# A sum built by its own DMA instead of copied, GpSimd's DMA order fixed, and one transfer for a row of reciprocals, in a two-layer non-local attention kernel

## Chip, cores, metric

The kernel runs on one core of a Trainium2 chip. The metric is the device time of one launch in microseconds, as the median of several runs. Tensor data are float32 throughout.

## What is computed

Two non-local (self-attention) blocks follow each other on `x` of shape 4 x 128 x 96 x 96 (batch, channels, height, width). One block, cut to its core:

```python
# x: (b, 128, 96, 96); CI = 64
g_x     = maxpool2(conv1x1(x, g_w, g_b)).reshape(b, CI, -1).transpose(0, 2, 1)
theta_x = conv1x1(x, theta_w, theta_b).reshape(b, CI, -1).transpose(0, 2, 1)
phi_x   = maxpool2(conv1x1(x, phi_w, phi_b)).reshape(b, CI, -1)
f = einsum('bqc,bck->bqk', theta_x, phi_x)       # 9216 queries x 2304 keys
y = einsum('bqk,bkc->bqc', softmax(f), g_x)
W_y = conv1x1(y, W_w, W_b)                       # then a batch norm with fixed statistics
return W_y * inv + (bn_beta - bn_mean * inv) + x
```

## The kernel before, in words

There are eight blocks (four images x two layers, in `ORDER`). A block's queries are cut into nine pairs of 1024, its keys into 18 tiles of 128. The main loop (L910) runs over 648 steps; one step is two key tiles of one pair, so nine steps make a pair and 18 steps, two pairs, make a cycle. In a step TensorE computes the scores of two key tiles (L592), ScalarE their exponentials with a fixed shift (L597), VectorE adds the exponentials up (L606, for the softmax's denominators), and TensorE multiplies the exponentials of the step before by the values (L614). There are six exponential buffers (`EXPS`).

Into these steps the kernel weaves two other works.

*The keys and values of the next block.* `g` and `phi` need a 1x1 convolution of x and a 2x2 max-pool. They are made in six units of 16 rows per block (class `Unit`, L400), by a scheme that saves multiplications: weights are combined once (`mixed`), and sums of x over halves of the channels and neighbouring rows are built by DMA. Two tiles hold sums, `sums[0]` (called `one`) and `sums[1]` (`two`); "low" and "high" are the partitions 0 to 63 and 64 to 127. `Unit.build` (L413) returns the steps:

- `load`: SP copies x into all of `one` and into `two[high]` (L422, L423);
- `add_one`: GpSimd issues two accumulating DMAs, x into both halves of `one` (L419);
- `load_rest`: SP copies x into `two[low]` (L426);
- an add of `one[high]` into `two[high]` (GpSimd, L419): the third sum;
- `copy_half` (L432): SP copies the second half of `two[high]`'s columns to `self.half`, 64 low partitions in a free part of the tile `stage` (L433), because TensorE shall read one half of the columns from the high and the other from the low partitions at the same time;
- an add of `two[high]` into `two[low]` (GpSimd, L419): the last sum.

TensorE uses these sums in four stages of a unit: `first` (x itself), `second` (L467, reads `two[high]`, first half of the columns) with `second_rest` (L470, reads `self.half`), `third` (reads `one`), `fourth` (reads `two[low]` and x). `second_rest` is emitted in the same step as `second`, after that step's scores and before the values (L946). The multiplications of `second` and `second_rest` both stand on L449, the others on L443.

The steps at which these pieces stand are written by hand. `UNITS` (L44) has the steps of the four stages and `BUILDS` (L45) those of `build`, for even and odd units, counted from the cycle of the unit's pair of units. An even unit builds at 10 to 15 and computes at 15, 16, 18 and 20; an odd one builds at 18 to 23 and computes at 25, 26, 28 and 30.

*The end of a pair.* When all keys of a pair are done, VectorE transposes and reduces the sum of exponentials (`turn`, L655), and `invert` (L670) makes the reciprocals. These are on 32 partitions and have to be spread along rows and over 64 partitions: four DMAs write them as rows into `stage` (L688, 1 KB each), four more broadcast each row over 64 partitions (L693, 64 KB each), all on SP. `normalise` (L703) multiplies by them, `multiply` (L705) projects, and `add` (L714) lets ScalarE add a shift and GpSimd add the result to x by an accumulating DMA (L724). In a cycle of 18 steps `invert` stands at step 13 for the even and at step 6 for the odd pair (`INVERT`), `normalise` at 1 and 10 (`NORM`), and the projection at 3 and 13 (`PROJECT`).

What sets the order: `tc.manual_schedule(engines=...)` (L99 to L101) keeps the program's order for TensorE, VectorE, ScalarE and SP. GpSimd is not in the set, and a scheduler places its instructions. Each engine takes its queue in order, and an instruction that waits holds all behind it. Semaphores carry the waits between engines and for landed DMAs.

```python
def second_rest(self):
    self.part(self.blk.w.mixed[:CI, 2, :], self.half, 1)
...
for i, step in zip(BUILDS[u % 2], unit.build()):
    later(cycle + u // 2 * CYCLE + i, step)
```

Of the kernel before, what the change touches and what calls it, by code (L numbers as in the profile page):

```python
# [17 lines left out]
B, C, CI, H, W = 4, 128, 64, 96, 96  # L18
HW = H * W
NK = (H // 2) * (W // 2)  # L20
QT = 512
# [18 lines left out]
UN = 4 * W  # L40
# [1 line left out]
UB = 2 * UK // 32  # L42
TB = NKT // 2
UNITS = ((15, 16, 18, 20), (25, 26, 28, 30))  # L44
BUILDS = ((10, 11, 12, 13, 14, 15), (18, 19, 20, 21, 23, 23))  # L45
STORE = 3
AFTER = ((1, 1, 2, 4, 5), (1, 2, 2, 3, 4))
THETAS = (6, 5)
# [4 lines left out]
SQ = 32  # L53
# [9 lines left out]
def shifted_blocks(ctx: ExitStack, tc: tile.TileContext, x: bass.AP, layers, out: bass.AP, flag):  # L63
# [24 lines left out]
    nc = tc.nc  # L88
# [8 lines left out]
    ps_misc = ctx.enter_context(tc.tile_pool(name="ps_misc", bufs=2, space=PSUM))  # L97

    engines = {mybir.EngineType.PE, mybir.EngineType.DVE, mybir.EngineType.Activation,  # L99
               mybir.EngineType.SP}  # L100
    ctx.enter_context(tc.manual_schedule(engines=engines))  # L101

    ident = const.tile([P, P], F32, name="ident")
# [10 lines left out]
    stage = const.tile([P, NK], F32, name="stage")  # L114
# [285 lines left out]
    class Unit:  # L400
# [12 lines left out]
        def build(self):  # L413

            low, high = slice(0, CI), slice(CI, P)
            one, two = sums

            def add(dst, src):
                nc.gpsimd.dma_start(out=dst, in_=src, accum_op=ALU.add)  # L419

            def load():
                nc.sync.dma_start(out=one, in_=self.pixels(0, slice(0, P)))  # L422
                nc.sync.dma_start(out=two[high], in_=self.pixels(1, low))  # L423

            def load_rest():
                nc.sync.dma_start(out=two[low], in_=self.pixels(1, high))  # L426

            def add_one():
                add(one[high], self.pixels(0, low))
                add(one[low], self.pixels(1, low))  # L430

            def copy_half():  # L432
                nc.sync.dma_start(out=self.half, in_=two[high, :, UN // 2 :])  # L433

            return (
                load, add_one, load_rest, lambda: add(two[high], one[high]), copy_half,
                lambda: add(two[low], two[high]),
            )

        def both(self, *some):  # L440
            for c in range(2):
# [107 lines left out]
    class Pair:  # L549
# [120 lines left out]
        def invert(self):  # L670

            four = work.tile(
                [SQ, P // SQ, SQ], F32, tag="four", name=f"four_{self.name}", bufs=1
            )
            both = work.tile([SQ, 2, SQ], F32, tag="both", name=f"both_{self.name}", bufs=1)
            for k in range(P // SQ):
                nc.vector.transpose(four[:, k, :], self.parts[ts(k, SQ), :])
            nc.vector.tensor_reduce(
                both[:, 0, :], four.rearrange("p k q -> p q k"), AX.X, ALU.add
            )  # L680
            nc.vector.reciprocal(both[:, 1, :], both[:, 0, :])
            nc.vector.tensor_reduce(notes[:SQ, self.number, :], both, AX.X, ALU.add)
            self.rc = self.halves[:, QT:]
            n = QT // SQ // 2
            first = CI + self.number % 2 * SQ
            for i in range(4):
                row = stage[first + i : first + i + 1, NK - UN :][:, : QT // 2]
                nc.sync.dma_start(  # L688
                    out=row.rearrange("o (b k) -> o b k", k=SQ), in_=both[ts(i, n), 1, :]
                )  # L690
            for i in range(4):
                row = stage[first + i : first + i + 1, NK - UN :][:, : QT // 2]
                nc.sync.dma_start(  # L693
                    out=self.rc[ts(i // 2, CI), ts(i % 2, QT // 2)],
                    in_=row.unsqueeze(1).to_broadcast([1, CI, QT // 2]),
                )

        def add_halves(self):
# [15 lines left out]
        def add(self):  # L714

            cols = ts(self.p, PT)
            here = self.blk.xt[:, cols]
            if self.number < late:
                for h in range(2):
                    nc.scalar.activation(  # L720
                        self.halves[:, ts(h, QT)], self.pss[h], AF.Identity,
                        bias=self.blk.w.shift,
                    )
                nc.gpsimd.dma_start(out=here, in_=self.halves, accum_op=ALU.add)  # L724
            else:
                for h in range(2):
                    dst = here[:, ts(h, QT)]
                    nc.vector.scalar_tensor_tensor(
                        dst, self.pss[h], self.blk.w.shift, dst, op0=ALU.add, op1=ALU.add
                    )  # L730
                self.put()
# [77 lines left out]
    def begin(n):  # L809

        blocks[n].xt = xs[ORDER[n][0]]
        blocks[n].begin_keys()
# [66 lines left out]
    def later(t, step):  # L879
        tails.setdefault(t, []).append(step)  # L880

    for n in range(1, len(blocks)):
        cycle = (n - 1) * NP * NB // CYCLE * CYCLE
        for u in range(NU):
# [5 lines left out]
            if u == 0:  # L890
                later(cycle + BUILDS[0][0], lambda n=n: begin(n))
            for i, step in zip(BUILDS[u % 2], unit.build()):
                later(cycle + u // 2 * CYCLE + i, step)
# [16 lines left out]
    for t in range(total + 1):  # L910
        q, s = 2 * (t // CYCLE), t % CYCLE
        even, odd = pairs[q : q + 2] if t < total else (None, None)
        first, second, take = None, *pending
# [3 lines left out]
        if t in keys:  # L917
            n, i = keys[t]
            first, *pending = blocks[n].chunks(i)
        elif unit:  # L920
            first = (unit.first, unit.second, unit.third, unit.fourth)[stage_of]
            second = unit.second_rest if stage_of == 1 else None
            take = (unit.first_sum, unit.second_sum, unit.third_sum, unit.fourth_sum)[stage_of]
        elif t < total and s == THETAS[q > 0]:
            if q < late:
                first, *pending = thetas(pairs[q + 1 : q + 3])
            else:
                first, take = odd.theta_alone()
# [342 lines left out]
def nonlocal_blocks(tc: tile.TileContext, x: bass.AP, layers, out: bass.AP):  # L1271
    with tc.tile_pool(name="flag", bufs=1) as pool:
        flag = pool.tile([1, 1], I32, name="flag")
        shifted_blocks(tc, x, layers, out, flag)
        bad = tc.nc.values_load(flag[0:1, 0:1])
        with tc.If(bad > 0):
            general_blocks(tc, x, layers, out)
# [30 lines left out]
```

## Time and profile before

| | us |
|---|---|
| median of three runs | 2748.55 (2744.99 to 2748.56) |
| the profiled execution, whole | 2745.14 |
| its span, first to last instruction | 2743.2 |
| TensorE busy | 2527.4 (92%) |
| VectorE busy | 2195.4 (80%) |
| ScalarE busy | 1667.2 (61%) |
| GpSimd busy | 213.5 (8%) |
| mean granted TensorE clock | 0.960 |

The profile is one execution, recorded by the hardware. PE is TensorE, DVE VectorE, ACT ScalarE, POOL GpSimd, SP the engine whose queue issues most DMAs; "PEld" is the loading of weights, which runs beside multiplications, and "SPq" or "POOLq" an engine's queue when it only issues. A tile is named without its number: `stage<-sums` is a transfer from a sums tile into `stage`. The releaser of a wait is inferred from semaphore events, so a wait on several things carries the name of the last. The issue of a DMA and its landing are two events: the row of an SP issue is the time in which SP issues, and the data arrive later. The granted clock is recorded in stretches at 1.00 or 0.50, which carry no reason.

### The profile page before, as it was taken

To read this page: it belongs to the slowest core of one execution; us is meant where nothing else is said; L and a number is where in the kernel's file an instruction comes from. 1 tells how busy PE (TensorE), PEld (TensorE's weight loads), DVE (VectorE), ACT (ScalarE), POOL (GpSimd) and SP (SyncE) were. 2 spreads that over 40 slices of the span, in tenths; PEclk is the share of its full clock that TensorE was granted. 3 is DMA by queue.
4 is the path that set the end of the run, shared out by engine and by line. 5 is a ranking of instruction groups with operands and counts; after the bars stand their busy time and mean duration, and the time that the engine had idled before them with its cause. 6 is when DMAs were issued, how large, how long until landed. Compare 5 with 4: busy or idle time off the path is not lost.

```text
span 2743.2 us, 56475 instructions
## 1 busy us (share of the span) xinstructions
PE 2527.4 (92%) x23391; PEld 1568.1 (57%) x23391; DVE 2195.4 (80%) x2947; ACT 1667.2 (61%) x1836; POOL 213.5 (8%) x244
## 2 busy tenths in 40 slices
PE   9888989889988898988998889898899888999998
PEld 4445544557744565455774456545566545666665
DVE  7777979778777796977876779787788677978877
ACT  5555656556655565755665556565566555666664
POOL 0010001100011000110001100010100110000000
PEclk9999999999999999999999999999999999999999
DMA  5355445443346444546334554444433455433333
GB/s 166 40 73 118 41 49 69 58 55 25 32 63 88 67 54 64 77 58 124 25 31 64 81 70 58 64 74 53 61 25 26 70 79 68 61 41 40 40 41 55
DMA packets 96980, 167.61 MB, mean 61 GB/s; under 512 B 17346, under 2 KB 74060, under 8 KB 96716
## 3 DMA queue, kind: packets, MB, share of 16 engines
q1 hardware_dynamic: 67652, 94.12, 27.9%
q0 software_dynamic: 28896, 69.75, 16.8%
q8 instruction: 185, 3.03, 0.4%
q14 instruction: 79, 0.65, 0.1%
q10 hardware_dynamic: 168, 0.07, 0.0%
HBM read 19.21 MB, written 18.87 MB: 14 GB/s over the span
## 4 chain that ended last, share of the span: by engine, by line
PE 68%; DVE 8%; DMA 7%; SPq 4%; issue 2%; ACT 2%; DVEq 0%; ACTq 0%
PE av L614 32%; PE sc L592 30%; DMA stage<-sums 5%; DVE sum L606 4%; SPq L693 4%; PE unit_ps L443 2%; PE theta_ps L269 2%; PE W_ps L709 2%; ACT exp L597 1%; DMA stage<-both 1%; DMA halves<-stage 1%; PE unit_ps L449 1%; DVE parts L665 1%; SPq L688 1%; DVE turned L664 1%
## 5 line engine op out<-in xcount | busy, mean ns | idle before, releaser
L597 ACT ACTIVATE exp<-sc,nshift 128x1024 f32<-128x1024 f32 x1296 | 1392.0, 1112 | 968.1 <-PE sc L592 929.4
L606 DVE TENSOR_TENSOR sum<-sum,exp 128x1024 f32<-128x1024 f32 x1151 | 1407.7, 1223 | 296.8 <-ACT exp L597 239.1
L592 PE MATMUL sc<-theta,phi 64*64 64x512 f32 x10368 | 1468.8, 593 | 3.0 <-ACT exp L597 2.9
L614 PE MATMUL av<-exp,gT 64*64 64x512 f32 x10368 | 1427.8, 604 | 0.0
L614 PEld LDWEIGHTS av<-exp,gT 64*64 64x64 f32 x10368 | 716.1, 136 | 411.2 <-issue 223.3
L592 PEld LDWEIGHTS sc<-theta,phi 64*64 64x64 f32 x10368 | 705.5, 134 | 410.5 <-issue 200.8
L449 PE MATMUL unit_ps<-stage,mixed 64*64 64x192 f32 x168 | 29.5, 433 | 189.1 <-DMA stage<-sums 189.1
L419 POOL DMA_DIRECT2D sums<-x x84 | 81.9, 1146 | 1280.0 <-PE sc L592 883.3
L724 POOL DMA_DIRECT2D x<-halves x70 | 66.1, 944 | 959.0 <-ACT halves L720 922.4
L476 DVE TENSOR_TENSOR stage<-stage,unit_ps 128x192 f32<-128x192 f32 x84 | 27.5, 349 | 138.7 <-PE unit_ps L449 138.7
L449 PEld LDWEIGHTS unit_ps<-stage,mixed 64*64 64x64 f32 x168 | 12.6, 167 | 217.2 <-issue 212.7
L604 DVE TENSOR_TENSOR sum<-exp,exp 128x1024 f32<-128x1024 f32 x72 | 88.1, 1223 | 33.1 <-ACT exp L597 33.1
L665 DVE TENSOR_REDUCE parts<-turned 128x16 f32<-128x512 f32 x142 | 97.4, 686 | 4.9
L664 DVE STREAM_TRANSPOSE turned<-sum 128x512 f32<-128x512 f32 x142 | 100.1, 705 | 0.5
L709 PE MATMUL W_ps<-halves,WT 64*64 64x512 f32 x568 | 91.9, 592 | 4.5 <-DVE halves L703 4.3
L621 ACT COPY halves<-av 128x1024 f32<-128x1024 f32 x71 | 71.9, 1013 | 35.4 <-PE av L614 35.4
L720 ACT ACTIVATE halves<-W_ps,shift 128x512 f32<-128x512 f32 x140 | 88.6, 692 | 0.7 <-PE W_ps L709 0.7
L269 PE MATMUL theta_ps<-x,thetaT 64*64 64x512 f32 x560 | 88.8, 589 | 0.0
L419 POOL DMA_DIRECT2D sums<-sums x84 | 68.7, 817 | 256.8 <-PE W_ps L709 86.0
L443 PE MATMUL unit_ps<-sums,mixed 64*64 64x384 f32 x504 | 79.2, 482 | 0.0
L503 DVE TENSOR_REDUCE stage<-stage 128x192 f32<-128x768 f32 x84 | 77.9, 941 | 0.0
L544 DVE STREAM_TRANSPOSE gT<-stage 32x192 f32<-32x192 f32 (+1 forms) x224 | 71.5, 319 | 3.8
(112 smaller groups left out, 851.1 us busy)
## 6 DMA issues: line engine op xcount, KB each, us to landing
x<-halves POOLq DMA_DIRECT2D x70, 512.0 KB, 4.7
halves<-stage SPq DMA_DIRECT2D x284, 64.0 KB
out_dram<-x SPq DMA_DIRECT2D x35, 512.0 KB
sums<-x SPq DMA_DIRECT2D x42, 384.0 KB
sums<-x SPq DMA_DIRECT2D x84, 192.0 KB
sums<-x POOLq DMA_DIRECT2D x84, 192.0 KB, 4.5
sums<-sums POOLq DMA_DIRECT2D x84, 192.0 KB, 3.8
x<-in_x_dram SPq DMA_DIRECT2D x18, 768.0 KB
```

The costliest lines, as they stand in the source:

```text
L269: nc.tensor.matmul(out, lhsT=lhsT, rhs=rhs, start=step == 0, stop=step == 1)
L419: nc.gpsimd.dma_start(out=dst, in_=src, accum_op=ALU.add)
L443: nc.tensor.matmul(bank[ts(c, CI), :UN], lhsT=lhsT, rhs=rhs[:, c, :], start=True, stop=True)
L592: nc.tensor.matmul(ps[ts(c, CI), ts(h, QT)], lhsT=self.blk.keys_of(k, c, h), rhs=self.th[ts(h, CI), :], start=True, stop=True,)
L597: nc.scalar.activation(e, ps, AF.Exp, bias=nshift)
L606: nc.vector.tensor_add(self.sum, self.sum, e)
L614: nc.tensor.matmul(self.av[ts(h, CI), ts(r, QT)], lhsT=self.blk.gT[ts(r, CI), k, :], rhs=e[ts(r, CI), ts(h, QT)], start=(k == 0), stop=(k ...
L664: nc.vector.transpose(self.turned, self.sum[:, ts(h, QT)])
L665: nc.vector.tensor_reduce(self.parts[:, ts(h, QT // SQ)], self.turned.rearrange("p (b k) -> p b k", k=SQ), AX.X, ALU.add,)
L693: nc.sync.dma_start(out=self.rc[ts(i // 2, CI), ts(i % 2, QT // 2)], in_=row.unsqueeze(1).to_broadcast([1, CI, QT // 2]),)
L709: nc.tensor.matmul(self.pss[h][ts(c, CI), :], lhsT=self.blk.w.W[ts(h, CI), ts(c, CI)], rhs=self.y[ts(h, CI), :], start=True, stop=True,)
L720: nc.scalar.activation(self.halves[:, ts(h, QT)], self.pss[h], AF.Identity, bias=self.blk.w.shift,)
```

## The change

1. The second half of the third sum gets its own load and its own add. `load` has a third transfer, of x into `self.half`; `add_two` adds `one[high]` into `self.half` on GpSimd and then, as before, into `two[high]`. `copy_half` goes. `build` returns five steps instead of six.
2. The steps change with it: in even units the add of the third sum stands at step 12 instead of 13 and the last add at 15 as before; in odd units at 20 instead of 21, and the last add at 22 instead of 23.
3. GpSimd joins the engines that keep the program's order. In the built program each unit's last add then stands behind the pair's L724 on GpSimd, where it stood ahead of it.
4. `invert` writes the four rows in one transfer of four partitions instead of four transfers. The four broadcasts stay.

```diff
-BUILDS = ((10, 11, 12, 13, 14, 15), (18, 19, 20, 21, 23, 23))
+BUILDS = ((10, 11, 12, 12, 15), (18, 19, 20, 20, 22))
...
     engines = {mybir.EngineType.PE, mybir.EngineType.DVE, mybir.EngineType.Activation,
-               mybir.EngineType.SP}
+               mybir.EngineType.SP, mybir.EngineType.Pool}
...
                 nc.sync.dma_start(out=two[high], in_=self.pixels(1, low))
+                nc.sync.dma_start(out=self.half, in_=self.pixels(1, low)[:, :, UN // 2 :])
...
-            def copy_half():
-                nc.sync.dma_start(out=self.half, in_=two[high, :, UN // 2 :])
-
-            return (
-                load, add_one, load_rest, lambda: add(two[high], one[high]), copy_half,
-                lambda: add(two[low], two[high]),
-            )
+            def add_two():
+                add(self.half, one[high, :, UN // 2 :])
+                add(two[high], one[high])
+
+            return load, add_one, load_rest, add_two, lambda: add(two[low], two[high])
...
-            n = QT // SQ // 2
             first = CI + self.number % 2 * SQ
+            rows = stage[first : first + 4, NK - UN : NK - UN + QT // 2]
+            nc.sync.dma_start(
+                out=rows.rearrange("r (b k) -> r b k", k=SQ), in_=both[:, 1, :]
+            )
             for i in range(4):
-                row = stage[first + i : first + i + 1, NK - UN :][:, : QT // 2]
-                nc.sync.dma_start(
-                    out=row.rearrange("o (b k) -> o b k", k=SQ), in_=both[ts(i, n), 1, :]
-                )
-            for i in range(4):
-                row = stage[first + i : first + i + 1, NK - UN :][:, : QT // 2]
                 nc.sync.dma_start(
                     out=self.rc[ts(i // 2, CI), ts(i % 2, QT // 2)],
-                    in_=row.unsqueeze(1).to_broadcast([1, CI, QT // 2]),
+                    in_=rows[i : i + 1, :].unsqueeze(1).to_broadcast([1, CI, QT // 2]),
                 )
```

## The prediction

> **What bounds the kernel now.** I read the page's busy row first, then the list of waits cut to PE, then the timelines of SP and GpSimd around one of those waits, then the windows with the granted clock, last the chain of waits behind it.
>
> The page's busy row and its group of L449 (busy us and mean ns of one | idle before it, and what ended that):
>
> ```profile
> PE 2527.4 (92%) x23391; PEld 1568.1 (57%) x23391; DVE 2195.4 (80%) x2947; ACT 1667.2 (61%) x1836; POOL 213.5 (8%) x244
> ...
> L449 PE MATMUL unit_ps<-stage,mixed 64*64 64x192 f32 x168 | 29.5, 433 | 189.1 <-DMA stage<-sums 189.1
> ```
>
> PE's longest waits (total us, times, longest):
>
> ```profile
> PE unit_ps L449 <- DMA stage<-sums: 189.1, 20, 11.3
> PE unit_ps L449 <- DMA sums<-sums: 10.5, 1, 10.5
> ```
>
> PE is busy 2527.4 of 2743.2 us and idle 215.8. Of that, 189.1 us are 20 waits of one matmul: `second_rest` (L470), which reads `self.half`, the copy that L433 makes by DMA. One more wait of 10.5 us is on `two[high]` itself. The rest is small (4.3 us at the very end for L703's y, 2.9 us for exponentials). So between these stops PE runs without a hole, and everything else is covered by it.
>
> Which units stop, and why, is in the queues. GpSimd's timeline, then SP's, for unit u=2 of the second block that is built (start, length, instruction):
>
> ```profile
> 463.89 1.94 POOL L419 DMA_DIRECT2D sums<-x  x2 [32.75 <-PE sc L592]
> 467.39 0.83 POOL L419 DMA_DIRECT2D sums<-sums  x1 [1.56 <-DMA sums<-x]
> 471.95 0.81 POOL L419 DMA_DIRECT2D sums<-sums  x1 [3.73 <-PE sc L592]
> 472.56 1.13 POOL L724 DMA_DIRECT2D x<-halves  x1
> ```
>
> ```profile
> 472.23 2.86 SPq L688 DMA_DIRECT2D stage<-both  x4
> 475.34 4.13 SPq L693 DMA_DIRECT2D halves<-stage  x4
> 479.52 2.35 SPq L433 DMA_DIRECT2D stage<-sums  x1
> ```
>
> The source of the copy, `two[high]`, was added from 467.39 and landed at 471.42. The copy leaves SP only at 479.52: step 14 stands behind `invert` (step 13), whose eight transfers SP issues in order. Then it shares the DMA engines with the four broadcasts of L693 and lands 8.3 us later. In an odd unit the copy (step 23) stands ahead of the next `invert` (step 24): it left at 427.55 and nobody waited. All 20 waits are even units; there are 21 (three in each of seven blocks), and the 21st is the 10.5 us one, beside a load of the next x.
>
> What the stop costs beyond its own length is in the windows (after the engines' busy times, PE to POOL, comes the granted clock) and in the chain:
>
> ```profile
> 479.40:488.00 8.60, 0.06 (x4) 0.09 (x5) 3.76 (x8) 1.11 (x1) 0.00 (x0) 0.63 0.71 35
> 488.00:491.60 3.60, 3.60 (x22) 2.48 (x26) 1.43 (x5) 0.00 (x0) 0.00 (x0) 0.50 0.00 0
> ```
>
> ```profile
> 473.70 4.11 DMA stage<-both
> ...
> 479.52 8.28 DMA stage<-sums
> 487.80 0.14 issue
> 487.94 0.58 PE unit_ps L449 x2
> ...
> 488.84 3.28 PE av L614 x14
> 492.12 1.72 PE sc L592 x16
> ```
>
> After the stop the granted clock is 0.50 for 3.6 us: 14 `av` matmuls take 3.28 us, where 16 take 1.72 a moment later. PE counts as busy there, so the 189.1 does not contain it.
>
> **The change part by part.**
>
> *The copy goes.* `second_rest` no longer waits for L433: minus 189.1 us, if the new `half` is there in time (next part).
>
> *The clock after the stops.* From the clock records: each of the 21 long stops is followed by 2.7 to 5.9 us at 0.50, 91.1 us together; work at half speed loses half, 45.5 us, of which 2.2 belong to the 21st stop. For twenty: minus 43.3. The Trainium skill (TensorE: Matmul & The Clock Gate, Part 1) says that the array falls to half clock after an idle window of some 3.4 us and comes back after some 3.4 us of work. By that rule twenty stops lose at most 20 x 1.7 = 34 us; the records say 43.3, and I take the records. The 4.3 us wait at 2723 was followed by no measurable half-speed work, so waits of 1 to 4 us that might remain cost little more than themselves.
>
> *The half built on its own.* Each of 42 units gets a load on SP (96 KB, 0.6 us as the `sums<-x` issues beside it) and an add on GpSimd (816 ns, the median of its 84 `sums<-sums`): 34 us of GpSimd, which is 8% busy. The bytes of load and copy are equal, the add's 96 KB are new. The load is last of three in step 10 (18), and behind it on SP stands `load_rest` 7 us later, so nobody is held. The add stands ahead of `add(two[high])` in GpSimd's queue and waits for the same landing of `one[high]`, so it starts where that one starts now (467.39), and `two[high]` 0.8 us later. Price of its landing, from both sides: 3.0 us (the last add of a unit alone) to 4.7 us (`two[high]` now), and 11.0 in the one unit where L693's broadcasts ran at the same time. I take 4. The cover: in 19 of the 20 units `two[high]` lands 4.0 to 7.6 us before `second` starts (median 6.3; 6.6 here; 36 in the very first) and `second_rest` is 1.3 us behind that. Less 0.8 for the queue and up to 1 for the added bytes, 2 to 6 us remain. So no wait: zero, with the end of the range at 2 us in each of the seven u=0 units (14 us). Below nothing it can't go. In the 21st unit the add meets the x load as before: 10.5 us stay, and the extra add lengthens them by 0 to 3; I take 1.5.
>
> *GpSimd in program order.* The built order shows one move, per unit: L724 (x<-halves) now stands ahead of the unit's last add. Behind L724's wait for ACT stands therefore that last add, and behind it `fourth`. L720 ends at 469.7, L724 can be issued then, and the last add, which waits for `two[high]` to land anyway (471.4 now, some 472.5 after), is not later than 473.5. It lands near 477.5 and `fourth` reads it near 493 (503.5 now less the stop): 15 us of cover. Zero. Odd units have 25 us or more.
>
> *One transfer for the reciprocals' rows.* 71 x 3 = 213 SP issues of 672 ns go, 2.0 us from each pair's row. The broadcasts still wait for the row to land: the chain shows 4.1 us for one row transfer, and the first L693 started 3.1 us after the first L688. So the four broadcasts end 0 to 2 us sooner. A rule speaks against it: the Trainium skill (DMA: Bandwidth & Descriptors, on why a DMA increments its semaphore by 16) lets a transfer use the largest number of engines up to 16 that divides the outermost sizes of both sides. That takes these rows from 8 engines with one run each to 4 engines with 8 runs each. By the trace's packet records a 128-byte packet takes 11 ns (median of those between 244 and 246 us), so eight in a row are 0.1 us, by the rule at most 0.1 us more than today; which engines carry them no view here shows. I take 0. L703 waited 27.9 us in all for these broadcasts, but on DVE, which is off the path, except 4.3 us for the last pair: minus 1 us there, between minus 2 and plus 1.
>
> *What is late next.* Without the stops DVE has 65.4 us of work (window 488.0 to 568.4) in a cycle of 80.4 - 8.5 - 2 = 70 us: 93%. From 443 to 479 it is already busy 35.1 of 36.4 us, with PE free of holes, its adds ending 1.3 to 3.4 us behind the exponentials. The six exponential buffers leave it 7 us more. In the stop it worked off 3.8 us; that moves to the next 18 us, where it is busy 55%. Zero, up to 1 us in each of 21 cycles.
>
> **The sum.** 2743.2 - 189.1 - 43.3 + 1.5 - 1 + 2 (small waits on DVE) = 2513.3 us of span. The profiled execution is 2745.14, 1.9 us more than its span: 2515. The median of the three runs, 2748.55, is 3.4 above it, the lowest 0.2 below; I add 2: 2517.
>
> **The rivals.**
>
> *A short wait stays or DVE takes over.* The adds share engines with L693 as in the 21st unit, or DVE at 93% falls behind. For: the 11 us landing there; DVE's 35.1 of 36.4. Against: `two[high]` lands before L693 starts in the other units; DVE is never waited for now. Price: 20 units x 1 to 4 us, 20 to 80 us, so 2537 to 2597. I give it 0.11.
>
> *The wait only changes its name.* If `half` always landed after L693's broadcasts it would arrive where the copy arrives now; 2740 to 2750. It needs the add to take 20 us in 20 units where `two[high]`'s took 3.8 to 5.1. 0.02.
>
> *Slower.* GpSimd's fixed order holds the last add behind L724, and `fourth` stops in all 42 units. Its cover is 15 us; each further us costs 42. To lose the 232 gained it must land 15 + 5.5 = 20.5 us late; from there it is slower than before, e.g. 2790 at 21.5. The issue above shows at most 1.5 us of delay. 0.03.
>
> **The numbers.** The forecast has 0.84, between 2505 (the 21st stop shrinks) and 2535 (u=0 waits and DVE's 21 us); the first rival's nearer part takes the range to 2550. Outside: about 0.1. 0.2% of this kernel, 5.5 us, is about what a measurement can tell from no change. Faster 0.95, same 0.02, slower 0.03.
>
> **What would show it.** Right: PE's list of waits has no wait on `stage` over 3 us in even units, PE idle near 30 us, PE busy near 2484, mean clock above 0.99, one stop near 10 to 13 us at the x load in the first block. Wrong: 20 waits on L449 with another releaser (`stage<-sums` from GpSimd, or `sums<-sums`); DVE's adds over 7 us behind ACT and PE waiting for exponentials; waits of `fourth` for `sums<-sums`.

## The result and the profile after

The changed kernel takes 2501.05 us (median of six runs, 2500.54 to 2501.78), the kernel before 2745.02 (six runs, 2742.11 to 2748.56). The ratio is 0.911, 95% interval 0.9098 to 0.9122. The forecast was 2517 with a range from 2505 to 2550: the direction and the mechanism of the twenty stops held, but the gain was some 16 us larger than the sum, and the time lies 4 us below the range, the largest part of this at the end of the last pair. The profiled execution took 2500.54, its span is 2498.8 and its mean granted clock 0.997.

From the page of the changed kernel, the busy row and the shares of the chain of work that ended last (where the copy stood, `half` now has its load on L424; the matmuls that waited are on L448):

```profile
PE 2474.1 (99%) x23391; PEld 931.2 (37%) x23391; DVE 2192.2 (88%) x2947; ACT 1671.2 (67%) x1836; POOL 254.6 (10%) x286
...
PE 93%; DVE 3%; DMA 2%; ACT 1%; SPq 1%; issue 1%; POOL 0%; DVEq 0%; POOLq 0%; ACTq 0%
```

PE's longest wait in the changed kernel (total us, times, longest):

```profile
PE unit_ps L448 <- DMA sums<-sums: 13.4, 1, 13.4
```

The row of 189.1 us in 20 waits is gone, one stop is left, and the chain that ended last is 93% PE, of 68% before. GpSimd's timeline for the unit that the prediction showed (u=2 of the second block built), then SP's:

```profile
433.53 0.95 POOL L419 DMA_DIRECT2D stage<-sums  x1 [1.55 <-DMA sums<-x]
434.12 1.22 POOL L419 DMA_DIRECT2D sums<-sums  x1
438.40 0.90 POOL L720 DMA_DIRECT2D x<-halves  x1 [3.06 <-DMA sums<-sums]
438.98 1.15 POOL L419 DMA_DIRECT2D sums<-sums  x1
```

```profile
440.30 0.70 SPq L685 DMA_DIRECT2D stage<-both  x1
444.41 3.53 SPq L689 DMA_DIRECT2D halves<-stage  x4
```

The half's add is issued at 433.53 and lands at 436.52; `two[high]` lands at 438.41. PE takes them without a hole, and the step with `second` and the step behind it run at full clock (the 1.00 is the granted clock):

```profile
445.50:449.30 3.80, 3.80 (x47) 1.78 (x42) 3.71 (x8) 3.02 (x3) 0.00 (x0) 1.00 0.77 28
449.30:452.70 3.40, 3.40 (x36) 1.18 (x32) 3.23 (x8) 2.12 (x2) 0.00 (x0) 1.00 0.82 27
```

To place the gain I cut both traces into the 648 steps, from the first score matmul of a step to that of the next, and subtracted:

| part of the span | us, after less before |
|---|---|
| step 16 and 17 of the 20 even units that stopped | -236.5 |
| of this, the waits themselves | -189.1 |
| of this, slower work behind them | -47.4 |
| steps 16 and 17 of the 21st unit | +2.2 |
| all other steps | -2.8 |
| from the last step's scores to the end | -7.0 |
| up to the first step | -0.3 |
| sum | -244.4 |

It is the difference of the spans, 2743.2 - 2498.8 = 244.4.

### The profile page after: what moved, and what is told of

Same layout as the page of the kernel before. It is cut to its first block, busy times and chain, and to the rows that moved or that the text cites. A ratio compares the mean times of both kernels' runs of the same rounds, so it can differ in the third digit from the quotient of the medians.

```text
span 2498.8 us, 56189 instructions
## 1 busy us (share of the span) xinstructions
PE 2474.1 (99%) x23391; PEld 931.2 (37%) x23391; DVE 2192.2 (88%) x2947; ACT 1671.2 (67%) x1836; POOL 254.6 (10%) x286
## 4 chain that ended last, share of the span: by engine, by line
PE 93%; DVE 3%; DMA 2%; ACT 1%; SPq 1%; issue 1%; POOL 0%; DVEq 0%; POOLq 0%; ACTq 0%
PE sc L591 42%; PE av L613 42%; PE unit_ps L442 3%; PE theta_ps L269 2%; PE W_ps L705 2%; DVE sum L605 1%; DMA halves<-stage 1%; DMA sums<-x 1%; PE unit_ps L448 1%; DMA sums<-sums 1%; PE gphi_ps L321 0%; ACT exp L596 0%; SPq L124 0%; SPq L689 0%; PE gphi_ps L269 0%
## 5 line engine op out<-in xcount | busy, mean ns | idle before, releaser
L591 PE MATMUL sc<-theta,phi 64*64 64x512 f32 x10368 | 1288.3, 590 | 3.0 <-ACT exp L596 2.9
L613 PE MATMUL av<-exp,gT 64*64 64x512 f32 x10368 | 1241.1, 589 | 0.0
L591 PEld LDWEIGHTS sc<-theta,phi 64*64 64x64 f32 x10368 | 415.8, 133 | 676.7 <-issue 612.9
L613 PEld LDWEIGHTS av<-exp,gT 64*64 64x64 f32 x10368 | 412.7, 133 | 684.4 <-issue 654.8
L720 POOL DMA_DIRECT2D x<-halves x70 | 63.5, 907 | 1050.6 <-ACT halves L716 1028.1
L419 POOL DMA_DIRECT2D sums<-sums x84 | 91.5, 1090 | 41.6 <-DMA sums<-sums 22.3
L705 PE MATMUL W_ps<-halves,WT 64*64 64x512 f32 x568 | 75.2, 590 | 0.2 <-DVE stage L497 0.2
L269 PE MATMUL theta_ps<-x,thetaT 64*64 64x512 f32 x560 | 74.2, 589 | 0.0
L442 PE MATMUL unit_ps<-sums,mixed 64*64 64x384 f32 x504 | 69.3, 482 | 0.0
L676 DVE STREAM_TRANSPOSE four<-parts 32x32 f32<-32x32 f32 x284 | 56.4, 198 | 2.9
L699 DVE TENSOR_TENSOR halves<-halves 128x512 f32<-128x512 f32 x71 | 48.6, 685 | 7.9 <-DMA halves<-stage 7.8
L696 DVE TENSOR_TENSOR halves<-halves 128x512 f32<-128x512 f32 x71 | 48.5, 684 | 0.0
```

Source lines behind the costliest of these rows:

```text
L269: nc.tensor.matmul(out, lhsT=lhsT, rhs=rhs, start=step == 0, stop=step == 1)
L442: nc.tensor.matmul(bank[ts(c, CI), :UN], lhsT=lhsT, rhs=rhs[:, c, :], start=True, stop=True)
L591: nc.tensor.matmul(ps[ts(c, CI), ts(h, QT)], lhsT=self.blk.keys_of(k, c, h), rhs=self.th[ts(h, CI), :], start=True, stop=True,)
L613: nc.tensor.matmul(self.av[ts(h, CI), ts(r, QT)], lhsT=self.blk.gT[ts(r, CI), k, :], rhs=e[ts(r, CI), ts(h, QT)], start=(k == 0), stop=(k ...
L705: nc.tensor.matmul(self.pss[h][ts(c, CI), :], lhsT=self.blk.w.W[ts(h, CI), ts(c, CI)], rhs=self.y[ts(h, CI), :], start=True, stop=True,)
```

## The experiments

Theory after the result: the 20 stops came from the copy's place in SP's queue; the remaining difference is the clock behind the stops and the end of the last pair. Rivals: that the copy had to be replaced, that GpSimd's order or the rows' transfer did part of it, that the slow work behind a stop has another cause than idleness. Each time below stands beside runs of the kernel before on the same chip (medians 2742.89 for the first four, 2743.02 for the last three). The changed kernel was not run beside them, so a distance of 2 us from its 2501.05 (ratio 0.9098 to 0.9122) is not shown by the medians.

| kernel | median us | ratio to before (95%) |
|---|---|---|
| rows_alone | 2732.85 | 0.9958 (0.9944 to 0.9972) |
| after_no_rows | 2509.72 | 0.9148 (0.9134 to 0.9162) |
| copy_early | 2498.81 | 0.9110 (0.9096 to 0.9124) |
| warm | 2719.69 | 0.9911 (0.9896 to 0.9927) |
| order_alone | 2770.63 | 1.0106 (1.0089 to 1.0123) |
| after_no_order | 2499.00 | 0.9112 (0.9097 to 0.9127) |
| load_later | 2486.43 | 0.9066 (0.9051 to 0.9081) |

**copy_early: the kernel before with the copy ahead of the reciprocals.**

```diff
-BUILDS = ((10, 11, 12, 13, 14, 15), (18, 19, 20, 21, 23, 23))
+BUILDS = ((10, 11, 12, 12, 12, 15), (18, 19, 20, 21, 23, 23))
```

> The kernel before with one tuple of step numbers changed: in even units the add of the third sum and the copy stand at step 12 instead of 13 and 14, so the copy is ahead of the reciprocals on SP. Copy, scheduler and four row transfers stay. Theory: the copy's place in SP's queue was the whole cost, so the twenty stops go here too and the time is within 10 us of the changed kernel plus the 6 us of the last pair: 2500 to 2515. Rival: the copy's own landing behind the add (a second DMA in the chain) costs; then even units keep waits of 2 to 5 us, 40 to 100 us above the changed kernel.

PE's longest waits of that kernel, then SP's timeline at the unit shown above:

```profile
PE W_ps L709 <- DVE halves L703: 4.2, 1, 4.2
PE unit_ps L449 <- DMA sums<-sums: 3.5, 1, 3.5
```

```profile
430.81 0.59 SPq L433 DMA_DIRECT2D stage<-sums  x1
431.58 2.80 SPq L688 DMA_DIRECT2D stage<-both  x4
```

2498.81 us: two step numbers alone bring the whole gain, with the copy, the scheduler and the four row transfers in place. No wait on `stage<-sums` is left, so the copy, behind the add in its chain, was never too slow. The theory stands; the rival falls. One of the two numbers moves the add, from 13 to 12, but in the traces of the 20 units it is issued at most 1.8 us earlier against its step (0.2 us in the unit shown), while the copy now leaves as its source lands, where it had left 8.1 us later. So it is the copy's place that counts. The parts are not quite those of the changed kernel: steps 16 and 17 of the 20 units are 236.5 us shorter here too, the wait of the last pair stays, with an end that is 6.5 us longer, and the stop at the x load is shorter (3.5 us in place of 13.4). At that stop SP holds the copy until `two[high]` has landed (228.34), so the broadcasts behind it leave only from 232.2 on, and the add lands 4.0 us after its issue. In the changed kernel the broadcasts left from 221.9 to 224.1, just ahead of that add (224.7), which took 14.0 us.

**rows_alone and after_no_rows: the rows' transfer added alone, and taken out alone.** The edit is the diff of `invert` above, into the kernel before and out of the changed one.

> Only the one transfer for the reciprocals' rows is put into the kernel before; copy and GpSimd's order stay. My theory after the result: the last pair's wait of 4.3 us on L703 goes and with it 1.7 us of half clock, and the twenty stops stay as they are, because the copy still leaves SP behind the four broadcasts; at most 2 us sooner each. So 6 us less, 2735 to 2741, PE idle near 200. Rival, the prediction's sum: 1 us less, tail wait of about 3 us still there. Second rival: SP free 2 us sooner brings the copy forward by 2 us in each of 20 units, 40 us less and more with the clock.

> The changed kernel with the four row transfers put back. My theory: the twenty stops stay gone, the last pair's wait of 4 us comes back with up to 1.7 us of half clock, so 2505 to 2508 against 2501. Rival: the rows' transfer is also what keeps the half in time, then short waits on L448 in even units come back and the time is above 2515.

PE's waits, rows_alone:

```profile
PE unit_ps L449 <- DMA stage<-sums: 179.2, 20, 9.9
PE unit_ps L449 <- DMA sums<-sums: 9.5, 1, 9.5
```

after_no_rows:

```profile
PE unit_ps L448 <- DMA sums<-sums: 14.6, 1, 14.6
PE W_ps L708 <- DVE halves L702: 4.4, 1, 4.4
```

Put in alone, the transfer brings 10 us (8 to 15 by the interval), more than both the 6 expected and the prediction's 1. The wait of the last pair is gone, and the part from the last step's scores to the end is 5.7 us shorter (20.4 for 26.1). The 20 stops stay, each 0.5 us shorter (179.2 for 189.1); the second rival had said 2 us each. Taken out, the changed kernel loses 8.7 us, by medians from two sessions (10 by the ratios, 0.9148 and 0.911); the last pair's wait returns with 4.4 us, its end is 7.5 us longer, and no wait returns on L448 in the 20 units. So this edit is worth 5.7 to 7.5 us at the end in both kernels, and it isn't what keeps the half in time. Why the last pair's broadcasts land so much sooner is settled only in part. By SP's timeline they start 1.9 us after the row's issue, where it was 2.9, and L703 starts at most 13.5 us after it, where it was 17.2. The start explains 1 us of it. For the rest the DMA packets show a difference: in the stretch from 3.1 to 12.0 us after the row's issue, 120 packets (0.45 MB) of GpSimd's queue, L724's add to x, move beside the broadcasts in the kernel before (36 to 138 in the other four kernels with four row transfers), and none or one in the four kernels with the single transfer. That this sharing is the cause is not tested.

**warm: the kernel before with TensorE kept busy in the stops.** The extra products are overwritten before they are read.

```diff
         def second_rest(self):
+            if self.u % 2 == 0 and self.name != f"{blocks[1].name}_4":
+                for i in range(24):
+                    self.part(self.blk.w.mixed[:CI, 2, :], sums[0][:CI, :, : UN // 2], 1)
             self.part(self.blk.w.mixed[:CI, 2, :], self.half, 1)
```

> The kernel before, with 24 pairs of extra matmuls in each of the twenty even units that stop, before second_rest, into PSUM that second_rest and third write anew; they take some 7.7 us of a stop of 8.3 to 11.3 us, so the stop stays as long as it was but TensorE isn't idle in it. It measures the clock after a stop by itself. By the sum of the prediction (half of the half-speed stretch behind each stop) 43 us less, by the steps' lengths in the two traces 47 us less: 2698 to 2702, mean clock above 0.99. Rival: what follows a stop is slow for another reason (pipeline, weights), then nothing is gained, 2740 to 2750.

23 us less, half of what either sum said. PE's timeline at one of the stops shows what it looks like when it works:

```profile
484.28 7.96 PE L449 MATMUL unit_ps<-sums,mixed 64*64 64x192 f32 x96
493.29 0.38 PE L449 MATMUL unit_ps<-stage,mixed 64*64 64x192 f32 x2 [1.04 <-DMA stage<-sums]
...
493.66 1.88 PE L617 MATMUL av<-exp,gT 64*64 64x512 f32 x14
495.08 2.19 PE L595 MATMUL sc<-theta,phi 64*64 64x512 f32 x16
```

The stop is as long as before, but 14 `av` matmuls behind it take 1.88 us, and the next scores start 1.8 us after its end; in the same timeline of the kernel before those took 3.52, and the scores started 3.5 us after the stop (487.94 to 491.43). Why only half: in 12 of the 20 units the records still show 3.4 to 6.8 us at 0.50, in 8 none. In these 8, steps 16 and 17 are 9.0 us longer than in the changed kernel on average, which is the stop alone; in the kernel before the same 8 units were 11.85 us longer with stops of 9.28. So where the clock stays up, nothing is lost behind the stop: 2.6 us per stop is the price there, and idleness its cause. The other 12 differ from the 8 in what was left of the wait once the extra products had run out: 1.4 to 3.5 us in the 12, 0.5 to 1.4 us in the 8. Longer filling, or filling that uses more of the array, was not tried.

**order_alone and after_no_order: GpSimd's program order added alone, and taken out alone.**

```diff
-               mybir.EngineType.SP}
+               mybir.EngineType.SP, mybir.EngineType.Pool}
```

> Only GpSimd's program order is put into the kernel before. There L724 (x<-halves) then stands ahead of the add of two[high] and of the last add in even units, so the copy's source lands some 3 us later, but the copy still leaves SP only at its place behind the broadcasts. Theory: within 5 us of the kernel before, 2740 to 2750. Rival: L724 ahead of the add makes the copy later, 20 units x 1 to 3 us, 2765 to 2805.

> The changed kernel with GpSimd left to the scheduler again. In the built order two[high]'s add then stands ahead of the half's, and the last add ahead of L720. Theory: both land with several us to spare, so within 2 us of the changed kernel's 2501. Rival: the half behind two[high] in the queue is late in the units with the smallest cover (u=0), 10 to 30 us more.

Added alone it is slower by 27.6 us; the theory fell, and the rival's size came, though not by the rival's way. GpSimd's and SP's timelines of order_alone at the unit of the stops above:

```profile
478.88 0.92 POOL L724 DMA_DIRECT2D x<-halves  x1 [4.12 <-ACT halves L720]
479.46 1.18 POOL L419 DMA_DIRECT2D sums<-sums  x1
486.51 0.80 POOL L419 DMA_DIRECT2D sums<-sums  x1 [5.87 <-issue]
```

```profile
481.22 3.81 SPq L688 DMA_DIRECT2D stage<-both  x4
485.59 3.70 SPq L693 DMA_DIRECT2D halves<-stage  x4
489.34 6.90 SPq L433 DMA_DIRECT2D stage<-sums  x1
```

With step 13 for the add of `two[high]`, program order puts it behind L724, which waits for ACT. It is issued 6.0 us behind the second add of x (473.42), where that was 2.9 us before, and takes 6.5 us to land, beside the 512 KB of L724, instead of 4.0.

Even so it has landed at 485.96, 3.4 us before the copy leaves SP at 489.34: the copy does not wait for its source. What is new beside the broadcasts and the copy is the unit's last add. It waits for `two[high]`, so it is issued at 486.51, amid the broadcasts, where it stood ahead of them before (471.95, landed at 475.95); SP now takes 6.90 us to issue the copy, and took 2.35. In each of the 19 units behind an L724, SP takes 4.8 to 7.0 us over one of these issues; in the first unit, which has no L724 ahead of it, the stop stays (9.1 us for 9.2). That the last add's bytes are what holds SP up is argued from these times, not tested.

The waits on `stage<-sums` grow from 189.1 to 209.6 us, the 21st from 10.5 to 15.0. In the changed kernel the add of `two[high]` stands at step 12, ahead of L724, there is no copy to hold up, and no even unit but the 21st stops. With the order taken out of it, the median is 2 us lower (2499.00; the ratio, 0.9112, is the same within its interval); the trace shows the difference in the one stop that is left, 10.8 instead of 13.4 us. The edit to GpSimd's order alone brings no gain that these runs show.

**load_later: the last stop.**

```diff
-    loads = {4 * NB + 7: 2, 31 * NB + 6: 3}
+    loads = {7 * NB + 6: 2, 31 * NB + 6: 3}
```

> The changed kernel with the load of the third x moved from step 43 to step 69, where no unit is being built. It is about the one stop that stays (13.4 us). Theory: the stop is the collision of the x load, and the broadcasts behind it, with the adds of unit u=4 of the first block; it goes with 1.5 to 3 us of half clock: 2484 to 2487, PE idle under 6 us. Rival: the adds are slow there for the broadcasts alone, then the stop stays and the time is 2501.

2486.43 us, 14.6 less than the changed kernel (12 by the ratios, 14.6 by the spans of the traces), as expected. The longest of PE's waits that are left:

```profile
PE sc L591 <- ACT exp L596: 3.2, 6, 1.2
```

No stop is left; PE's waits are 6.0 us together, of 208.8 before. Steps 16 and 17 of the 21st unit became 14.6 us shorter. There the x load had held the build back: the adds of x are now issued 16.6 us ahead of step 16 instead of 3.4, and the third sum has landed before the broadcasts leave. copy_early has the other half: with the broadcasts held back instead, the late add took 4.0 us and the stop 3.5. So the long stop needed both, the load and the broadcasts. This is the fastest kernel of the study. copy_early with the rows' transfer and the later load, without the half's own sum and without GpSimd's order, should reach the same by the parts above; it was not run.

## Why the prediction came out as it did

*What bounds the kernel, and where the stops came from:* right. 189.1 us of waits were predicted to go and went. copy_early shows the cause to be the copy's place in SP's queue.

*The half in time:* right. The half's add took 3.0 us to land in the unit shown (4 was taken). In the 20 units the half lands 7.7 us or more before `second_rest`, and `two[high]` 5.1 us or more before `second`, where 2 to 6 had been left. No u=0 unit waits.

*GpSimd in program order, within this change:* right at zero. The last add is issued 4.9 us behind `two[high]`'s (5.3 by the prediction's times) and is read 15.3 us after it lands (15 predicted). It took 6.8 us to land, beside L720's transfer, and not 4.0. The slower rival's hold was real, though not in this kernel: in order_alone the last add is held, but `fourth` never waits for it; the time is lost at the copy.

*DVE next:* right that it isn't the bound, at 88%. The 2 us put in for it did not come, and the other steps became 2.8 us shorter instead, for no reason that these runs show: 4.8 us of the error. (Its 55% was read from the stretch behind the stop before, 407.1 to 425.0; behind the stop shown, from 488.0 to 506.0, it is 59%. Nothing rests on it.)

*The clock behind the stops:* the mechanism was right, the size too small. 43.3 us were predicted from half of the half-speed stretches, 47.4 is what the steps became shorter beyond the waits. The Trainium skill's rule (TensorE: Matmul & The Clock Gate, Part 1: half clock after an idle window of about 3.4 us, full again after as much work) would have given at most 34, by the prediction's estimate from it; the steps show more, 2.4 us a stop. 4.1 us of the error.

*The end of the last pair:* this step failed, in both its terms, and is the largest part of the error. The prediction said that the 4.3 us wait "was followed by no measurable half-speed work", and that the rows' transfer would bring 1 us there. PE's timeline of the kernel before, against that of the changed one:

```profile
2723.43 1.30 PE L709 MATMUL W_ps<-halves,WT 64*64 64x512 f32 x8 [4.33 <-DVE halves L703]
2724.48 3.45 PE L614 MATMUL av<-exp,gT 64*64 64x512 f32 x16
```

```profile
2481.41 1.03 PE L705 MATMUL W_ps<-halves,WT 64*64 64x512 f32 x8
2482.27 1.89 PE L613 MATMUL av<-exp,gT 64*64 64x512 f32 x16
```

Sixteen matmuls take 3.45 us after the wait and 1.89 without it. The half-speed stretch begins at 2724.2, 0.8 us after the wait's end; I had looked only for one that had begun within it. The whole end is 7.0 us shorter where 1 was predicted, 6.0 us of the error, and rows_alone shows that this edit does it (5.7 us there). The wait and the slow matmuls behind it are some 6 of the 7 us.

*The 21st stop:* it stayed, 13.4 us long for the 12.0 predicted.

*The sum.* Of the span, 14.5 us were missed: 6.0 at the end, 4.8 in the allowance for DVE and other steps, 4.1 in the clock, 0.3 at the start, less 0.7 at the 21st stop. From span to median I added 3.7 us and it was 2.3, another 1.4. All but one have the same sign, which the range did not allow for: it reached 12 us below the forecast and 33 above it, although each of the small costs above it had been argued to be zero; its low end stood for a shorter 21st stop, which did not come.

## What to carry to other kernels

Before work is rebuilt to arrive sooner, look at what stands ahead of it on its queue: here two step numbers did what a new load, a new add and a changed scheduler did. Fixing an engine's order is only as good as the step numbers that it then follows; the same setting cost 28 us where it pushed the adds behind a waiting transfer into the broadcasts, and nothing that these runs show where they stood ahead of it. A stop of TensorE is priced with the half-speed work behind it, also a short one, and also when the slow stretch starts a little after the stop has ended.

## What was not expected of the hardware

A wait of 4.3 us sufficed for 3.4 us at half clock, which began only after the wait. In the clock records of the kernel before, all 23 half-speed stretches begin on one grid of 3.41 us (within 5 ns) and all but the last, which the end of the run cuts, end on it. Those of the 21 stops last two to four steps of it (6.8, 10.2 or 13.7 us, much of it within the stop), that behind the last pair's wait one. So the clock changed only at these marks, which fits the spread of 2.7 to 5.9 us behind the stops. Stops filled with 64 x 64 matmuls still left a half-speed stretch in 12 of 20 cases, those with 1.4 to 3.5 us of idleness at their end.

The accumulating DMA of 192 KB that makes the third sum landed in 3.8 to 5.0 us in 20 of the 21 even units of the kernel before, and in 5.9 to 6.9 us in the 19 units of order_alone where it was issued 0.6 us behind one of 512 KB on the same queue; next to the broadcasts of single rows and behind a load of x it took 14.0 us in the changed kernel.
